# The last sequence of an attention and gated-network kernel: the order of its counts, and its third gate piece in two halves

## The chip, the cores and the metric

The kernel runs on one core of one Trainium2 chip. The metric is the device time of a run in microseconds (us); three runs of the kernel before are given, and their median is what the kernel after is compared with. All profiles here are of one execution of the program on that core.

The five engines work beside each other, each on its own queue of instructions in order: TensorE (PE in the profile, its weight loads PEld), VectorE (DVE), ScalarE (ACT), GpSimd (POOL) and SyncE (SP), which here issues most DMAs.

## What is computed

The reference, cut to what matters (B = 8 sequences of T = 512 places, E = 256, 16 heads of 16):

```python
xn = layernorm(x)
# attention: rotary positions on q and k, causal, at most 250 places back
q, k, v = split(xn @ in_proj_w.T)
attn = softmax(where(mask, rope(q) @ rope(k).T * 16 ** -0.5, min))
s = (attn @ v) @ out_proj_w.T
# gated network: weights of +1 and -1 from boolean arrays
h = s0 * (concat([xn, -xn]) @ pm1(k0));  h = relu(h) * 2
h = s1 * (h @ pm1(k1));                  h = relu(h) * 2
h = s2 * (h @ pm1(k2))
out = x + s * silu(h)
```

So the output needs, for each sequence, the attention's projection s, the gate g = h * sigmoid(h), and x itself.

## The kernel before, in words

Everything is laid out with features on the 128 partitions and the 512 places in the free dimension. Per sequence the kernel normalizes x, projects q, k and v, applies the rotation, and works through nine attention steps; each takes scores on TensorE, exponentials on ScalarE, masks on GpSimd, and the products with v on TensorE. A column of ones beside v gives the softmax sums. Meanwhile the gated network runs on TensorE: `layer` (lines 502 to 530) makes one 128-row block of h1 or h2 from a high part (16 bit) and a low part. Its `high` is a ScalarE instruction (L529) and its `low` a VectorE instruction (L527). `last` (lines 554 to 601) makes the final product z of the network, two blocks of 128 features.

**The order of the work.** The instructions of all engines are written in one order, worked out by a planner, `run` (lines 226 to 242). Pieces of TensorE work lie on a time axis with a cost each; sorted by place, they advance a clock. A piece returns follow-up steps with a delay; a step is put out as soon as the clock has passed its due time, before the next piece. A step that itself returns steps counts their delays from its own due time. Delays thus set the order in every engine's queue, and nothing is moved between queues. Each engine works its queue in that order.

**The last sequence.** In sequence 7 the network's second layer is done in two halves of 256 columns, and its output in four pieces u = 0 to 3 (`outputs`, lines 532 to 535): u = 0 and 1 are the two feature blocks of the first half of the columns, u = 2 and 3 those of the second. The pieces differ in how the gate is made:

- u = 0 and 1: `scale` (L597) copies z out of PSUM, and `gate_ready` (lines 620 to 637) follows at 7.5 and 11.0 planner units: an exponential on ScalarE (L624), an addition of 1 on GpSimd (`add`, L628), two half-width reciprocals on VectorE (`invert_`, L633), and a product on GpSimd (L635).
- u = 2 and 3 ("final"): `ends` is an exponential (L584) and an addition of 1 (L585), both on ScalarE; `ready` is one reciprocal over 256 columns (L589) and a product with z (L590), both on VectorE. The buffer `den` of u = 2 takes the place of that of u = 0 and 1 (`beside`, lines 537 to 547: one buffer per tag, pieces with odd u take the right half). The first exponential of u = 2 therefore waits until L635 of u = 1 has read it.

**The divisions.** `divisions` (lines 959 to 969) plans, for each of the two head pairs of a sequence, four reciprocals of softmax sums (`invert`, L884), and then `divide` (lines 886 to 906): a shuffle on VectorE (L890), and 2.0 units later `product` on GpSimd (L893), which divides V. `below` on GpSimd (L897) compares the sums S with a least value, and `count` on VectorE (L902) counts the sums in range into a column of `counts`. In the last sequence `below` comes 0.0 after `product`, and `count` 1.5 after `below`.

**The check and the fallback.** `add_up` (lines 973 to 978) sums all counts: a product with ones on TensorE (L975, into a PSUM buffer of the same three that the projections use), a VectorE reduction (L977) and a cast (L978). At the end all engines read that number (L1025) and branch (L1072): if a sum was out of range, a plain version of the whole computation runs; with these inputs it doesn't.

**The end.** `project_o` (lines 908 to 948) makes the attention's projection for each u on TensorE (L916). For u = 0 and 3 VectorE multiplies it with the gate straight from PSUM (L938) and the residual is added on GpSimd or VectorE (L945); for u = 1 and 2 ScalarE copies it out of PSUM (L928), GpSimd multiplies (L929), and VectorE (u = 1) or GpSimd (u = 2) adds the residual (L931). Then the piece is stored, by SyncE's queue or, for u = 3, ScalarE's.

In the last sequence the places on the planner's axis, in order, are: h2 blocks f = 0 to 7 of the second half, the product of u = 2, `add_up`, the product of u = 3, and `project_o` of u = 0, 1, 2, 3. `add_up` and the steps cost the planner's clock nothing; an h2 block costs 1.725, a product of `last` 1.87, a `project_o` 0.87. The first gate product of this sequence (u = 0) is followed by the last attention step (1.7), the gate product of u = 1 (1.87), block f = 0, the last attention products (0.7), and blocks f = 1 to 7. The `divide` of the second pair stands between blocks f = 3 and f = 4.

Of the kernel before, what the change touches and what calls it, by code (L numbers as in the profile page):

```python
# [15 lines left out]
AF = mybir.ActivationFunctionType  # L16
ALU = mybir.AluOpType
# [17 lines left out]
def tile_attention_times_gated_ffn(  # L35
# [42 lines left out]
    nc = tc.nc  # L78
    P = 128
    B, T, E = x.shape  # L80
# [90 lines left out]
    scales = const.tile([P, 2], F32, name="scales")  # L171
# [360 lines left out]
    def outputs(b):  # L532

        n = 1 if b + 1 < B else 2
        return [(f, ts(half, T // n)) for half in range(n) for f in range(EC)]

    def beside(b, u, tag):

        st = states[b]
        if b + 1 == B and u % 2:  # L540
            return st[tag][:, T // 2 :]
        if b + 1 == B and u == 2 and tag == "xr":

            st[tag] = turned.tile([P, 2, T], F32, tag="mb", name=f"xr_{b}_{u}", bufs=1)[:, 0]
        else:
            st[tag] = work.tile([P, T], F32, tag=tag, name=f"{tag}_{b}_{u}", bufs=1)
        return st[tag][:, : T // 2] if b + 1 == B else st[tag]

    def residual(b, u):
        f, cols = outputs(b)[u]  # L550
        xr = states[b]["xr", u] = beside(b, u, "xr")
        nc.sync.dma_start(xr, x_t[b, ts(f, P), cols])

    def last(b, u, how):
        st = states[b]
        f, cols = outputs(b)[u]
        if how == "final":
            pz = ps_s.tile([P, 2, T], F32, tag="sc", name=f"z_ps_{b}_{u}")[:, 0, : T // 2]
        else:
            pz = ps_m.tile([P, T], F32, tag="mm", name=f"z_ps_{b}_{u}")  # L560
            if b + 1 == B:
                pz = pz[:, : T // 2]
        if how == "at once":
            for c in range(NF1):
                nc.tensor.matmul(
                    pz, w2["l"][:, c, ts(f, P)].bitcast(F32), st["h2p"][:, c, cols],
                    start=(c == 0), stop=(c == NF1 - 1),
                )
        else:
            for p in "hl":  # L570
                for c in range(NF1):
                    nc.tensor.matmul(  # L572
                        pz, w2[p][:, c, ts(f, P)], st["h2" + p][:, c, cols],
                        start=(c == 0 and p == "h"), stop=(c == NF1 - 1 and p == "l"),
                    )
        if cols.start == 0:
            st["gate of", f] = outs.tile([P, T], F32, tag=f"gate{f}", name=f"gate_{b}_{f}")
        gate = st["gate", u] = st["gate of", f][:, cols]
        if how == "final":
            residual(b, u)  # L580
            den = beside(b, u, "den")

            def ends():
                nc.scalar.activation(den, pz, AF.Exp, scale=scales[:, 1:2])  # L584
                nc.scalar.activation(den, den, AF.Identity, bias=1.0)  # L585
                return [(0.0 if u == 2 else 0.88, ready)]

            def ready():
                nc.vector.reciprocal(den, den)  # L589
                nc.vector.scalar_tensor_tensor(  # L590
                    gate, pz, scales[:, 0:1], den, ALU.mult, ALU.mult
                )

            return [(0.0, ends)]

        def scale():
            nc.vector.tensor_scalar(gate, pz, scales[:, 0:1], None, ALU.mult)  # L597
            if how != "later":
                return [(7.5 if u == 0 else 11.0, lambda: gate_ready(b, u))]

        return [(0.0, scale)]
# [18 lines left out]
    def gate_ready(b, u):  # L620
        st = states[b]
        residual(b, u)
        gate, den = st["gate", u], beside(b, u, "den")
        nc.scalar.activation(den, gate, AF.Exp, scale=-1.0)  # L624
        width = T // 2 if b + 1 == B else T

        def add():
            nc.gpsimd.tensor_scalar(den, den, 1.0, None, ALU.add)  # L628
            return [(0.9 + 1.1 * k, lambda k=k: invert_(k)) for k in range(2)]

        def invert_(k):
            part = den[:, ts(k, width // 2)]
            nc.vector.reciprocal(part, part)  # L633
            if k == 1:
                return [(1.8, lambda: nc.gpsimd.tensor_tensor(gate, gate, den, ALU.mult))]  # L635

        return [(0.5, add)]
# [17 lines left out]
    def finish_ffn(b, u, how):  # L655
        quick.add(last_at(b, u))
        out = [(last_at(b, u), L3 * (2 if b + 1 < B else 1), lambda: last(b, u, how))]
        if how == "later":
            out.append((late(b, u) - 4.5, 0, lambda: gate_ready(b, u)))
        return out  # L660
# [225 lines left out]
    def divide(b, pair):  # L886
        st = states[b]
        V, S = st["V", pair], st["S", pair]
        R = turned.tile([P, 2, T], F32, tag="hi", name=f"R_{b}_{pair}")[:, 0]
        nc.vector.stream_shuffle(R, S, [(n + D) % 32 for n in range(32)])  # L890

        def product():
            nc.gpsimd.tensor_tensor(V, V, R, ALU.mult)  # L893
            return [(3.0 if b + 1 < B else 0.0, below)]

        def below():
            nc.gpsimd.tensor_scalar(R, S, 1 / MOST, None, ALU.is_ge)  # L897
            return [(4.0 if b + 1 < B else 1.5, count)]

        def count():  # L900
            n = 2 * b + pair
            nc.vector.scalar_tensor_tensor(  # L902
                R, S, 1 / LEAST, R, ALU.is_le, ALU.mult, accum_out=counts[:, n : n + 1]
            )

        return [(2.0, product)]
# [241 lines left out]
```

## Time and profile before

| what | value |
|---|---|
| three runs, median (lowest to highest) | 607.96 us (607.72 to 608.24) |
| profiled execution, span from first to last instruction | 607.0 us |
| profiled execution's own time beyond the span | not stated by the profile |
| granted TensorE clock, mean | 0.995 |
| instructions | 11176 |
| VectorE's last instruction of the work (L945) | 600.25 to 600.74 us |
| idle of ScalarE before L584 of u = 2, released by GpSimd L635 | 2.06 us |
| L584 with 256 columns (exponential) | 473 ns |
| L585 with 256 columns (addition of 1 on ScalarE) | 416 ns |
| L589 with 256 columns (reciprocal) | 1729 and 1753 ns |
| L884 with 128 columns (reciprocal) | 893 to 954 ns |
| L897 with 512 columns (comparison on GpSimd) | 1491 to 1822 ns |
| L902 with 512 columns (count) | 681 to 940 ns |

How to read it: the span runs from the first to the last instruction of one execution, so it is a little shorter than a run's time. The timeline and the chain give starts in microseconds from the span's start. An idle time in front of an instruction names what released it; it is inferred from semaphore events. Where two timeline rows of one engine overlap by a few hundredths, the engine has them in its pipeline together.

### The profile page before, as it was taken

How to read it: one execution, taken by the hardware profiler on the slowest of the kernel's cores; microseconds unless marked ns; L12 is line 12 of the kernel's file. 1: busy time of each engine (PE TensorE's matmuls, PEld its weight loads, DVE VectorE, ACT ScalarE, POOL GpSimd, SP SyncE). 2: the span in 40 equal slices, each digit the busy share in tenths (PEclk: the TensorE clock that was granted, in tenths of full speed). 3: DMA queues.
4: the chain of work that ended last, by engine and by line, in shares of the span. 5: the costliest groups of instructions: out<-in, count | busy, mean ns of one | idle time of the engine just before them, and what ended most of it. 6: DMA issues, size and time to landing. Idle time of an engine off the chain costs nothing. (4 is left out here: it accounts for less than half of the span.)

```text
span 607.0 us, 11176 instructions
## 1 busy us (share of the span) xinstructions
PE 594.8 (98%) x4492; PEld 367.2 (60%) x4492; DVE 383.5 (63%) x606; ACT 294.7 (49%) x414; POOL 309.0 (51%) x368
## 2 busy tenths in 40 slices
PE   7999999999999999999999999999999999999994
PEld 6654666555655556556565566555666555657783
DVE  6864637558467485665856657666666557554774
ACT  4676664354554535445453454542554445555321
POOL 2975542466533663445724557235662456627632
PEclk9999999999999999999999999999999999999998
DMA  8552722226331443315243252421642216222201
GB/s 273 216 187 94 272 87 88 86 106 207 105 122 53 176 138 105 122 65 216 85 134 108 106 210 78 142 94 70 210 131 94 88 69 243 71 65 77 71 1 41
DMA packets 38061, 74.51 MB, mean 123 GB/s; under 512 B 5360, under 2 KB 13040, under 8 KB 38000
## 3 DMA queue, kind: packets, MB, share of 16 engines
q1 hardware_dynamic: 35568, 71.48, 34.0%
q10 hardware_dynamic: 2432, 2.23, 1.2%
q8 instruction: 37, 0.61, 0.4%
q14 instruction: 24, 0.20, 0.1%
HBM read 44.30 MB, written 29.39 MB: 121 GB/s over the span
## 5 line engine op out<-in xcount | busy, mean ns | idle before, releaser
L752 ACT ACTIVATE p<-sc 128x1024 f32<-128x1024 f32 (+2 forms) x144 | 138.3, 1012 | 74.9 <-PE sc L733 45.1
L768 POOL TENSOR_SCALAR_AFFINE_SELECT p<-p 128x512 f32<-128x512 f32 x128 | 91.3, 719 | 127.4 <-ACT p L752 127.4
L518 PE MATMUL h_ps<-h1l,w1l_sb 128*128 128x512 f32 (+1 forms) x576 | 146.2, 396 | 0.0
L518 PE MATMUL h_ps<-h1h,w1h_sb 128*128 128x512 f16 (+1 forms) x576 | 123.1, 356 | 0.0
L518 PEld LDWEIGHTS h_ps<-h1l,w1l_sb 128*128 128x128 f32 x576 | 100.2, 188 | 29.5 <-issue 9.2
L529 ACT ACTIVATE h2h<-h_ps 128x512 f16<-128x512 f32 (+1 forms) x72 | 39.4, 548 | 112.6 <-PE h_ps L518 112.6
L518 PEld LDWEIGHTS <-w1h_sb 128*128 128x128 f16 x576 | 51.2, 98 | 58.8 <-issue 17.5
L775 POOL TENSOR_SCALAR_AFFINE_SELECT p<-p 128x512 f32<-128x512 f32 (+1 forms) x96 | 49.3, 513 | 71.4 <-ACT p L752 71.4
L807 PE MATMUL po<-p,v_pad 128*32 128x378 f32 (+4 forms) x1216 | 76.5, 372 | 0.0
L633 DVE RECIPROCAL den<-den 128x256 f32<-128x256 f32 (+1 forms) x32 | 52.5, 1644 | 24.9 <-POOL den L628 24.9
L733 PEld LDWEIGHTS sc<-q,k 32*128 32x128 f32 x1216 | 44.2, 184 | 30.4 <-issue 21.1
L527 DVE SCALAR_TENSOR_TENSOR h2l<-h_ps,h2h 128x512 fp32r<-128x512 f32 (+1 forms) x72 | 43.8, 609 | 29.6 <-ACT h2h L529 29.6
L527 DVE SCALAR_TENSOR_TENSOR h1l<-h_ps,h1h 128x512 fp32r<-128x512 f32 x64 | 42.7, 680 | 25.7 <-ACT h1h L529 25.6
L733 PE MATMUL sc<-q,k 32*128 32x378 f32 (+4 forms) x1216 | 58.1, 306 | 0.6 <-DMA q<-dq 0.3
L884 DVE RECIPROCAL S<-S 128x128 f32<-128x128 f32 x64 | 57.5, 920 | 0.1
L518 PE MATMUL h_ps<-xl,w0l_sb 128*128 128x512 f32 x128 | 52.3, 489 | 0.0
L807 PEld LDWEIGHTS po<-p,v_pad 128*32 128x32 f32 x1216 | 31.7, 109 | 28.4 <-issue 17.0
L529 ACT ACTIVATE h1h<-h_ps 128x512 f16<-128x512 f32 x64 | 38.0, 598 | 18.7 <-PE h_ps L518 18.6
L301 DVE TENSOR_TENSOR xT<-xT,of_all 128x512 f32<-128x512 f32 x28 | 22.3, 801 | 28.4 <-DMA of_all<-d 27.9
L518 PE MATMUL h_ps<-xh,w0h_sb 128*128 128x512 f16 x128 | 38.4, 382 | 0.1
L572 PE MATMUL z_ps<-h2l,w2l_sb 128*128 128x512 f32 (+1 forms) x144 | 36.1, 391 | 0.2 <-DVE h2l L527 0.2
L425 POOL TENSOR_TENSOR m_ka<-m_ka,m_kb 128x512 f32<-128x512 f32 x16 | 20.1, 1276 | 28.5 <-DVE m_kb L404 28.5
(101 smaller groups left out, 735.1 us busy)
## 6 DMA issues: line engine op xcount, KB each, us to landing
q<-dq SPq DMA_DIRECT2D x64, 256.0 KB, 3.5
dq<-qh SPq DMA_DIRECT2D x16, 512.0 KB, 3.1
dq<-m_qa SPq DMA_DIRECT2D x16, 512.0 KB, 5.5
k<-dk SPq DMA_DIRECT2D x32, 256.0 KB, 2.7
dk<-kh SPq DMA_DIRECT2D x8, 512.0 KB, 2.9
dk<-m_ka SPq DMA_DIRECT2D x8, 512.0 KB, 2.9
x<-in_x_dram SPq DMA_DIRECT2D x30, 128.0 KB, 2.7
xT<-in_x_t_dram SPq DMA_DIRECT2D x7, 512.0 KB, 5.6
```

The costliest lines, as they stand in the source:

```text
L301: nc.vector.tensor_tensor(xT, xT, st["of_all"][:, i], op)
L518: nc.tensor.matmul(ph, w[p][:, c, ts(f, P)], st[src + p][:, c, cols], start=(k == 0), stop=(k == n - 1),)
L527: nc.vector.scalar_tensor_tensor(lo, ph, 0.0, hi, ALU.max, ALU.subtract)
L529: high = lambda: nc.scalar.activation(hi, ph, AF.Relu)
L572: nc.tensor.matmul(pz, w2[p][:, c, ts(f, P)], st["h2" + p][:, c, cols], start=(c == 0 and p == "h"), stop=(c == NF1 - 1 and p == "l"),)
L633: nc.vector.reciprocal(part, part)
L733: nc.tensor.matmul(sc[r // 2][:, r % 2, ds(off, n)], st["k0", g][row, ts(j, P)], st[f"q{turn}", g][row, ds(j * P + first, n)], start=(turn ...
L752: nc.scalar.activation(p[:, 2 * half : 2 * half + 2, :n], sc[half][:, :, :n], AF.Exp, scale=D ** -0.5,)
L768: nc.gpsimd.affine_select(out=block, in_=block, compare_op=ALU.is_ge, fill=0.0, base=0, pattern=[[0, 4], [1, P]], channel_multiplier=-1,)
L775: nc.gpsimd.affine_select(out=block, in_=block, compare_op=ALU.is_ge, fill=0.0, base=-1, pattern=[[0, 4], [-1, beyond]], channel_multiplier=1,
L807: nc.tensor.matmul(po[32 * r : 32 * r + 32, ds(j * P + first, n)], v_columns(j, g, r), p_[:, r, ds(off, n)], start=(j == 0), stop=(done an ...
L884: nc.vector.reciprocal(part, part)
```

## The change

Three delays and one step of the last sequence change; other sequences keep their instructions and their order.

- In `product` and `below`, for the second pair (pair = 1) of the last sequence, the delay before `below` goes from 0.0 to 2.5 and that before `count` from 1.5 to 2.5. The first pair keeps 0.0 and 1.5.
- `ends` of u = 2 makes two exponentials of 128 columns on ScalarE and no addition. `ready` of u = 2 makes, for each half, the addition of 1 on VectorE and then the reciprocal. u = 3 stays as it was.
- `ready` of u = 2 comes 0.1 after `ends` instead of 0.0. `add_up`, which has the next place on the axis, is then put out ahead of `ready`.

```diff
+            halves = [ts(k, T // 4) for k in range(2)]
+
             def ends():
+                if u == 2:
+                    for k in halves:
+                        nc.scalar.activation(
+                            den[:, k], pz[:, k], AF.Exp, scale=scales[:, 1:2]
+                        )
+                    return [(0.1, ready)]
                 nc.scalar.activation(den, pz, AF.Exp, scale=scales[:, 1:2])
                 nc.scalar.activation(den, den, AF.Identity, bias=1.0)
-                return [(0.0 if u == 2 else 0.88, ready)]
+                return [(0.88, ready)]
 
             def ready():
-                nc.vector.reciprocal(den, den)
+                if u == 2:
+                    for k in halves:
+                        nc.vector.tensor_scalar(den[:, k], den[:, k], 1.0, None, ALU.add)
+                        nc.vector.reciprocal(den[:, k], den[:, k])
+                else:
+                    nc.vector.reciprocal(den, den)
                 nc.vector.scalar_tensor_tensor(
                     gate, pz, scales[:, 0:1], den, ALU.mult, ALU.mult
                 )
...
         def product():
             nc.gpsimd.tensor_tensor(V, V, R, ALU.mult)
-            return [(3.0 if b + 1 < B else 0.0, below)]
+            return [(3.0 if b + 1 < B else 2.5 * pair, below)]
 
         def below():
             nc.gpsimd.tensor_scalar(R, S, 1 / MOST, None, ALU.is_ge)
-            return [(4.0 if b + 1 < B else 1.5, count)]
+            return [(4.0 if b + 1 < B else 1.5 + 1.0 * pair, count)]
```

## The prediction

> **What bounds the kernel now.** I read the page's busy shares first, then the chain that ended last in order of time, then the timeline of the last 18 us, then the end-of-program entries of the trace.
>
> The busy shares (busy us, share of the span, instructions):
>
> ```profile
> PE 594.8 (98%) x4492; PEld 367.2 (60%) x4492; DVE 383.5 (63%) x606; ACT 294.7 (49%) x414; POOL 309.0 (51%) x368
> ```
>
> TensorE carries the kernel until the matmuls run out. All that the diff touches lies in the last sequence, after about 586 us, where the order is different. The chain (start us, us, what):
>
> ```profile
> 589.11 1.36 POOL den L628
> 590.47 2.24 issue
> ...
> 593.49 0.48 ACT den L584
> ...
> 594.51 1.76 DVE den L589
> ...
> 600.25 0.49 DVE gate L945
> ```
>
> See that the chain begins on GpSimd, not on TensorE: the second gate's addition (L628) is late, its two reciprocals (L633) and multiplication (L635) follow, and only then does ScalarE start the third piece's exponential (L584), since it overwrites the den buffer that L635 reads. From 594.51 to 600.74 VectorE works with no gap. Why L628 is late, and what else stands in a row, is in the timeline (start us, us, engine, line, operation):
>
> ```profile
> 587.54 1.49 POOL L897 TENSOR_SCALAR R<-S 128x512 f32<-128x512 f32 x1
> ...
> 589.06 0.69 DVE L902 SCALAR_TENSOR_TENSOR R<-S,R 128x512 f32<-128x512 f32 x1 [2.36 <-POOL R L897]
> ...
> 592.92 0.38 PE L572 MATMUL z_ps<-h2l,w2l_sb 128*128 128x256 f32 x1 [0.20 <-DVE h2l L527]
> ...
> 596.92 1.59 PEld L916 LDWEIGHTS att_ps<-V,wo_sb 128*128 128x128 f32 x8 [0.23 <-DVE found_f L977]
> ```
>
> The comparison L897 holds GpSimd until 589.03 although L628's input is there at 586.26 (ScalarE L624, 585.85 + 0.41). The count L902 waits for L897 and holds up the lows (L527) behind it; at 592.92 TensorE itself waits 0.20 for the last low, and at 596.9 another 0.23 for L977, whose PSUM buffer it needs. After the last addition the program branches around its fallback:
>
> ```profile
> L1072 DVEq COMPARE_BRANCH  x1: 76/76/76, 601.0 to 601.0; - x1
> L1072 SPq COMPARE_BRANCH  x1: 45/45/45, 601.2 to 601.2; - x1
> L1072 ACTq COMPARE_BRANCH  x1: 54/54/54, 601.7 to 601.7; - x1
> ...
> L1072 DVEq EVENT_SEMAPHORE  x1: 21/21/21, 605.6 to 605.6; - x1
> L1072 ACTq EVENT_SEMAPHORE  x1: 17/17/17, 605.7 to 605.7; - x1
> ```
>
> So 6.26 us (600.74 to 607.0) follow VectorE's last instruction: a store (issue 0.37 from 600.78), the branch, about 4 us until the engines go on, and the closing.
>
> **What the Trainium skill says.** (1) "SBUF — State Buffer", section "SBUF: two separate sides": a VectorE instruction with two SBUF inputs and a GpSimd one exclude each other. The trace agrees: L628 with 256 columns took 0.85 in its first run and 1.36 beside L902. (2) "VectorE: DVE Perf Modes", "The perf-mode tier table": a 32-bit tensor_scalar in SBUF can go at two elements a cycle. The trace's nearest, L311 (256 columns, operands from SBUF), took 0.41, and L256 with 2 to 4 columns 0.17, which is one a cycle; none with an immediate and many columns on VectorE, in SBUF, is in the trace. (3) "Runtime: NRT & Kernel Launch", "Instruction fetch mechanics": a taken branch out of the fetched window waits for a DMA of instructions. The trace agrees: 2.8 to 4.6 us from branch to next entry (GpSimd 600.1 to 602.9, VectorE 601.0 to 605.6).
>
> **Part 1: comparison and count later (L897, L902).** I followed the planner's clock by hand. With c the clock after the h2 pieces f5, f6, f7 (16.49, 18.215, 19.94 in units counted from the last sequence's first gate piece), product is due at 15.04, the second gate's addition at 16.94, its reciprocals at 17.84 and 18.94, its multiplication at 20.74. Before: comparison 15.04, count 16.54. After: 17.54 and 20.04. So GpSimd's order becomes L893, L628, L897, L635, and the count passes low f5, L633, low f6, L633, low f7 on VectorE; 20.04 against 19.94 is a thin but certain order. Nothing is added or dropped, and no DMA moves.
> GpSimd: L893 ends 587.45, L628 587.54 to 588.39 (0.85, as no L902 is beside it; 1.36 if a low disturbs it), L897 588.4 to 589.9 (1.49; the trace has up to 1.82). VectorE: low f5 at 587.81 (its high ends 587.78) instead of 589.7; L633 588.42 to 589.37; low f6 after the high of f6 (589.22 + 0.38): 589.63 to 589.99; L633 to 590.96; low f7 after high f7 (591.05 + 0.38): 591.46 to 591.82; count 591.8 to 592.5 with its accumulator read. L635 runs 591.1 to 591.8. Thus TensorE no longer waits at 592.7: z of u=2 ends at 591.66 + 1.18 = 592.84, and ScalarE starts at 592.87 instead of 593.49. The work that hides L897 now is the lows and reciprocals up to 591.8; 1.9 us of slack, so even 1.36 for L628 and 1.82 for L897 (+0.84) cost nothing. Behind the count wait the sum matmul L975 and behind it z of u=3: TensorE reaches L975 at about 592.7, the counts are there at about 592.55. Cover 0.1 to 0.2 only; a slow L902 (longest in the trace 0.94, +0.25) would push L975 and L977 by about 0.1.
>
> **Part 2: sum ahead of the reciprocals (L975, L977, L978).** The third piece's ready step gets a delay of 0.1 and so falls past add_up: L977 and L978 now come before it. L975 at 592.7 to 592.95, L977 593.0 (0.16), L978 593.2 to 593.31, next VectorE instruction at 593.33. The first exponential half is ready at 593.24, so this costs 0.06 to 0.1 in front and takes L977 and L978 out of the row between L590 and L938: L590 to L938 was 0.67 (596.30 to 596.97), and becomes about the 0.40 of L590's pitch, gain 0.27. TensorE's 0.23 wait for L977 goes too. L975 and z of u=3 move up by about 0.55, so its exponential (now 595.40) starts at 594.83 and its den is ready at 595.8.
>
> **Part 3: the third piece in halves.** ScalarE loses L585 (0.42) and has two exponentials of 128 columns: L529 gives 0.384 at 256 and 0.596 at 512 columns, so 0.106 less than L584's 0.473, 0.367 each; first one 592.87 to 593.24, second done by 593.6. VectorE gains two additions and has two reciprocals for one. Additions: not in the trace at this size. Lower bound 0.17 (L256, nearly no columns), upper 0.41 (L311, double columns); I take 0.27, near 0.29 for one element a cycle. Reciprocals: 0.90 each (L884 pairs, 1.76 for two) against 1.75. So L590 starts at 593.33 + 2 x (0.27 + 0.04 + 0.90 + 0.02) = 595.79, against 596.30: gain 0.51.
> The second half's exponential is hidden under the first half's reciprocal (0.9 against 0.37). The halves count as apart: at 595.40 ScalarE wrote the other half of this same buffer while L589 was at work.
>
> **Sum.** 0.51 up to L590 and 0.27 behind it: 0.78 at L938. Then L589 of u=3 needs its den at 596.5 (there at 595.8), L931 needs GpSimd's L929, whose row starts with L938 as before and whose copies come from a TensorE that is 0.5 to 0.8 earlier: no new wait. L945 ends 599.96 instead of 600.74. The stores and the branches of SP, VectorE and ScalarE move by the same 0.78, if the tail keeps its 6.26. The trace doesn't state its execution's own time; span 607.0 lies 0.96 under the median of the three runs, 607.96 (607.72 to 608.24), and I keep that 0.96 for what is around it. Span 606.22, time **607.2**, that is 0.13% less.
>
> **Rivals.**
> A, the forecast: 0.4 to 1.1 us off, 606.85 to 607.55. The ends are the additions' bounds (0.17 gives 0.98, 0.41 gives 0.50) and 0.1 for the count.
> B, the VectorE row eats most of it: additions of 0.41, reciprocals of 0.95 as two of L633 were, the count 0.2 late, or halves that wait for both exponentials (0.3). Gain 0.1 to 0.3, time 607.75. For it: the thin cover of the count. Against: the 0.17 fixed part leaves little room.
> C, slower: the branch. Counts summed early let TensorE and SP read the total sooner, and TensorE, GpSimd, VectorE and ScalarE branch in other places between the stores. One restart took 4.6, another 2.8; an engine that now takes 4.0 and meets the stores' packets (16 DMA engines up to 90% busy at 601 to 602.7) can take longer. From 0.78 more on it eats the gain; with 1.5 more, 608.7. Against: all these fetches already lie among stores, and all shift together.
> D, the same spread the other way: ScalarE and VectorE restart in about 3 us, as GpSimd did. One more us off: 606.2.
>
> **Numbers.** A 0.62, B 0.20, C 0.08, D 0.10. The range, 606.7 to 608.1, holds A and B and leaves out most of C and D. Chances of faster by over 0.2% (1.2 us, about what a measurement of this kernel can tell from no change; under 606.74): 0.11, D and a rest of A. Slower by over 0.2% (over 609.2): 0.03, the far part of C. Within: 0.86.
>
> **What would show it.** L628 starts before L897 at about 587.5; TensorE's wait at 592.9 is gone; the first L584-like exponential starts at 592.9, released by TensorE and not by L635; L977 starts at about 593.0, and no L916 wait for it; L590 of u=2 starts at about 595.8, L938 at 596.2, L945 ends at about 600.0. If additions measure over 0.45, or L977 starts after 593.4, B holds. If L945 ends at 600.0 but the span is not near 606.2, it is C or D. The prediction is wrong at its root if ScalarE's third exponential still waits for L635.

## The result, and the profile after

The kernel after takes 607.11 us (median of 21 runs, 606.51 to 608.32), the kernel before 607.85 (21 runs beside them). The ratio is 0.9985 with a 95% interval of 0.9979 to 0.9990: 0.1% to 0.2% faster. Forecast were 607.2 and a range of 606.7 to 608.1. Two later measurements of the same pair gave 0.9978 (0.9969 to 0.9987) and 0.9984 (0.9978 to 0.9991). The gain is small, but all three intervals leave out no change.

The profiled execution of the kernel after has a span of 604.9 us and a time of 606.62. Its busy shares hardly differ from before:

```profile
PE 593.5 (98%) x4492; PEld 366.9 (61%) x4492; DVE 384.1 (64%) x609; ACT 294.2 (49%) x414; POOL 312.9 (52%) x368
```

The diff adds 13 lines in front of all that follows it, so L897, L902, L628, L977, L938, L945 and L1072 of before are L910, L915, L641, L990, L951, L958 and L1085 here. In the step of u = 2 the exponentials are L588, the additions L599, the reciprocals L600 and the product L603. The timeline of the kernel after (start us, us, engine, line, operation, idle before it and releaser):

```profile
587.19 0.86 POOL L641 TENSOR_SCALAR den<-den 128x256 f32<-128x256 f32 x1
588.13 1.49 POOL L910 TENSOR_SCALAR R<-S 128x512 f32<-128x512 f32 x1
...
590.64 1.05 PE L572 MATMUL z_ps<-h2h,w2h_sb 128*128 128x256 f16 x8
...
591.44 1.18 PE L572 MATMUL z_ps<-h2l,w2l_sb 128*128 128x256 f32 x8
...
592.20 0.08 DVE L915 DVE_READ_ACCUMULATOR R<-S,R 128x1 f32 x1
...
592.56 0.21 PE L988 MATMUL total<-counts,ones 128*1 128x24 f32 x2
...
592.72 0.62 ACT L588 ACTIVATE den<-z_ps,scales 128x128 f32<-128x128 f32 x2 [1.50 <-PE z_ps L572]
...
592.80 0.17 DVE L990 TENSOR_REDUCE found_f<-total 1x1 f32<-1x24 f32 x1 [0.52 <-PE total L988]
593.01 0.14 DVE L991 CAST whole<-found_f 1x1 int32<-1x1 f32 x1
593.12 0.23 DVE L599 TENSOR_SCALAR den<-den 128x128 f32<-128x128 f32 x1
593.38 0.95 DVE L600 RECIPROCAL den<-den 128x128 f32<-128x128 f32 x1
594.25 0.16 DVE L599 TENSOR_SCALAR den<-den 128x128 f32<-128x128 f32 x1
594.45 0.95 DVE L600 RECIPROCAL den<-den 128x128 f32<-128x128 f32 x1
595.44 0.48 DVE L603 SCALAR_TENSOR_TENSOR gate<-z_ps,scales,den 128x256 f32<-128x256 f32 x1
595.84 0.41 DVE L951 TENSOR_TENSOR gate<-att_ps,gate 128x256 f32<-128x256 f32 x1
...
599.14 0.50 DVE L958 TENSOR_TENSOR gate<-gate,xr 128x256 f32<-128x256 f32 x1
```

The same places before:

```profile
590.86 1.05 PE L572 MATMUL z_ps<-h2h,w2h_sb 128*128 128x256 f16 x8
...
593.49 0.47 ACT L584 ACTIVATE den<-z_ps,scales 128x256 f32<-128x256 f32 x1 [2.06 <-POOL gate L635]
...
596.30 0.48 DVE L590 SCALAR_TENSOR_TENSOR gate<-z_ps,scales,den 128x256 f32<-128x256 f32 x1
596.70 0.16 DVE L977 TENSOR_REDUCE found_f<-total 1x1 f32<-1x24 f32 x1
...
596.97 0.40 DVE L938 TENSOR_TENSOR gate<-att_ps,gate 128x256 f32<-128x256 f32 x1
```

See four things. The addition L641 runs ahead of the comparison and takes 0.86, not 1.36. The eight matmuls of z stand in one piece of 1.18, where before the eighth waited for a low. ScalarE's exponential is released by TensorE and no longer by GpSimd's product. And L990 and L991 lie in front of the gate's additions, so that L951 can follow L603 at once.

The executions start their last part at different times, so I measure from the first matmul of z of u = 2. From there to the end of the last addition it is 599.64 - 590.64 = **9.00** us, against 600.74 - 590.86 = **9.88** before. This "distance" has lost 0.88, and what lies behind the last addition went from 6.26 to 604.9 - 599.64 = 5.26. The second of these needs its own explanation, since the change has nothing in it that should shorten the end. The end of the kernel after, in the entries of its branch:

```profile
L1085 SPq COMPARE_BRANCH  x1: 45/45/45, 599.8 to 599.8; - x1
L1085 DVEq COMPARE_BRANCH  x1: 76/76/76, 599.8 to 599.8; - x1
L1085 ACTq COMPARE_BRANCH  x1: 54/54/54, 600.7 to 600.7; - x1
...
L1085 DVEq EVENT_SEMAPHORE  x1: 21/21/21, 603.1 to 603.1; - x1
L1085 ACTq EVENT_SEMAPHORE  x1: 17/17/17, 604.0 to 604.0; - x1
```

VectorE goes on 3.3 after its branch, not 4.6 as before; ScalarE 3.3, not 4.0.

### The profile page after: what moved, and what is told of

The parts are those of the page before. It is cut to its first block, busy times and chain, and to the rows that moved or that the text cites. A ratio compares the mean times of both kernels' runs of the same rounds, so it can differ in the third digit from the quotient of the medians.

```text
span 604.9 us, 11178 instructions
## 1 busy us (share of the span) xinstructions
PE 593.5 (98%) x4492; PEld 366.9 (61%) x4492; DVE 384.1 (64%) x609; ACT 294.2 (49%) x414; POOL 312.9 (52%) x368
## 4 chain that ended last, share of the span: by engine, by line
PE 94%; DVE 2%; POOL 1%; DMA 1%; ACT 0%; issue 0%; ACTq 0%; DVEq 0%
PE h_ps L518 48%; PE po L820 12%; PE z_ps L572 9%; PE sc L746 9%; PE v_ps L365 4%; PE att_ps L929 4%; PE ka_ps L388 2%; PE qa_ps L388 2%; PE kb_ps L388 2%; PE qb_ps L388 2%; DMA wqkv_sb<-in_w_qkv_dram 1%; POOL m_qa L425 1%; POOL m_ka L425 0%; POOL w1l_sb L194 0%; DVE m_qa L449 0%
## 5 line engine op out<-in xcount | busy, mean ns | idle before, releaser
L781 POOL TENSOR_SCALAR_AFFINE_SELECT p<-p 128x512 f32<-128x512 f32 x128 | 94.9, 748 | 125.7 <-ACT p L765 125.6
L897 DVE RECIPROCAL S<-S 128x128 f32<-128x128 f32 x64 | 57.5, 920 | 0.1
L301 DVE TENSOR_TENSOR xT<-xT,of_all 128x512 f32<-128x512 f32 x28 | 23.7, 848 | 26.1 <-DMA of_all<-d 25.6
```

The source lines that it names most:

```text
L781: nc.gpsimd.affine_select(out=block, in_=block, compare_op=ALU.is_ge, fill=0.0, base=0, pattern=[[0, 4], [1, P]], channel_multiplier=-1,)
```

## The experiments

All profiles in one table, in us; "end" is from the end of the last addition to the end of the span.

| kernel | first matmul of z, u = 2 | distance | end | span |
|---|---|---|---|---|
| before; again; a third time | 590.86; 591.28; 591.05 | 9.88; 9.89; 9.87 | 6.26; 5.73; 5.08 | 607.0; 606.9; 606.0 |
| order alone | 590.62 | 9.34 | 5.24 | 605.2 |
| sum alone | 590.78 | 9.64 | 5.58 | 606.0 |
| halves alone | 590.81 | 9.86 | 6.13 | 606.8 |
| order and sum | 590.61 | 9.08 | 5.61 | 605.3 |
| after; again; a third time | 590.64; 591.65; 590.76 | 9.00; 9.00; 9.00 | 5.26; 5.35; 5.24 | 604.9; 606.0; 605.0 |
| late count | 590.76 | 10.38 | 5.86 | 607.0 |
| tangent | 591.05 | 8.48 | 5.47 | 605.0 |
| tangent, store by SyncE | 590.57 | 8.49 | 5.94 | 605.0 |
| no branch | 591.52 | 9.00 | 2.78 | 603.3 |

My theory: VectorE's row (its instructions one behind the other) in the last ten microseconds carries the gain, term by term (theory 1). The first rival: the gain is scatter in the engines' restart after the branch. The second: of the three parts, one gives nothing.

### Order alone

```diff
-            return [(3.0 if b + 1 < B else 0.0, below)]
+            return [(3.0 if b + 1 < B else 2.5 * pair, below)]
-            return [(4.0 if b + 1 < B else 1.5, count)]
+            return [(4.0 if b + 1 < B else 1.5 + 1.0 * pair, count)]
```

> Part 1 alone: the second pair's comparison and count later (delays 2.5 and 2.5), nothing else. Measure: the distance from the first matmul of z of u = 2 to the end of the last addition L945, 9.88 us before (590.86 to 600.74) and 9.00 after (590.64 to 599.64). Theory 1, the row of VectorE carries the gain: the exponential of u = 2 is released by TensorE at about 2.05 and not by L635 at 2.63, everything behind it moves by about 0.6, distance 9.26 to 9.3, time about 0.6 below the kernel before. Rival, the gain is scatter of the restart after the branch: the distance still shrinks, but the time stays within 0.2 of before.

Distance 9.34, so 0.54 off; the exponential starts 2.08 after the first matmul of z, released by TensorE:

```profile
592.70 0.47 ACT L584 ACTIVATE den<-z_ps,scales 128x256 f32<-128x256 f32 x1 [1.50 <-PE z_ps L572]
```

The gain is 0.04 to 0.08 less than theory 1 said. The time doesn't settle it: median 607.72 against 608.07 in these runs, 0.35 less, but a ratio of 1.0006 (0.9997 to 1.0015), whose interval leaves out a gain of 0.54 us (0.9991). I take the distance as shown, and what reaches the time from this part alone as open.

### Sum alone

```diff
-                return [(0.0 if u == 2 else 0.88, ready)]
+                return [(0.1 if u == 2 else 0.88, ready)]
```

> Part 2 alone: ready of u = 2 gets the delay 0.1, so the sum of the counts (L977, L978) comes ahead of the reciprocal; order of the comparison and the one whole reciprocal as before. Theory 1: L977 and L978 run while VectorE waits for ScalarE anyway (it idles 1.65 before L589), so they leave the row at no cost: distance 9.60, time 0.25 to 0.3 below before; TensorE's 0.23 wait for L977 is gone. Rival: the sum now waits for TensorE or for the counts and takes the place in front of the reciprocal, distance 9.85 or more, no gain.

Distance 9.64, 0.24 off, 0.04 less than theory 1 said. The ratio of 1.0004 (0.9994 to 1.0014) can't tell 0.24 us from nothing (median 607.95 against 608.07). The sum of this kernel runs under ScalarE's work:

```profile
593.40 0.17 DVE L977 TENSOR_REDUCE found_f<-total 1x1 f32<-1x24 f32 x1 [0.61 <-PE total L975]
593.61 0.14 DVE L978 CAST whole<-found_f 1x1 int32<-1x1 f32 x1
594.44 1.75 DVE L589 RECIPROCAL den<-den 128x256 f32<-128x256 f32 x1 [0.69 <-ACT den L585]
```

VectorE still idles 0.69 for L585 after the cast: here the sum costs nothing.

### Halves alone

The kernel after with the delays of before; the diff is against the kernel after:

```diff
-                    return [(0.1, ready)]
+                    return [(0.0, ready)]
-            return [(3.0 if b + 1 < B else 2.5 * pair, below)]
+            return [(3.0 if b + 1 < B else 0.0, below)]
-            return [(4.0 if b + 1 < B else 1.5 + 1.0 * pair, count)]
+            return [(4.0 if b + 1 < B else 1.5, count)]
```

> Part 3 alone: halves of u = 2 with the additions on VectorE; comparison, count and sum ordered as before. Theory 1: the first half's exponential (0.37 in place of 0.47 + 0.42) lets VectorE start 0.55 sooner, but two additions (0.23 and 0.16) and 0.14 more of reciprocals with their gaps follow on VectorE: L590 comes 0.05 to 0.15 sooner, distance 9.75 to 9.85, time within 0.2 of before. Rival, the halves are the main gain as the prediction's part 3 has it when it credits them with 0.5 at L590: distance 9.4 to 9.5.

Distance 9.86: 0.02 off, about the scatter of the distance itself and a little under the 0.03 to 0.13 that theory 1 gave. The time shows no gain either (ratio 1.0005, 0.9998 to 1.0011). The rows of this kernel:

```profile
593.83 0.23 DVE L599 TENSOR_SCALAR den<-den 128x128 f32<-128x128 f32 x1 [1.02 <-ACT den L588]
...
596.23 0.48 DVE L603 SCALAR_TENSOR_TENSOR gate<-z_ps,scales,den 128x256 f32<-128x256 f32 x1
```

VectorE starts 3.02 after the first matmul of z, where the whole reciprocal of before started at 3.65, 0.63 later. But it needs 2.40 until the product and not 1.79. The halves move ScalarE's addition onto the engine that is in short supply. Alone they give nothing that can be measured, as the second rival has it.

### Order and sum, without the halves

The edits of the first two kernels together.

> Parts 1 and 2 without part 3 (one exponential, the addition on ScalarE, one whole reciprocal). Theory 2: with L977 and L978 in front of it VectorE can't begin before about 2.48 in either form, and whole it ends as soon: exponential 2.08 to 2.55, addition to 3.0, reciprocal 3.05 to 4.8, L590 at 4.82 against 4.80 in the kernel after. Distance 9.0 to 9.05, time equal to the kernel after within 0.2, so the halves give nothing. Rival, the halves count: distance 9.3 or more and time 0.3 to 0.5 above the kernel after.

Distance 9.08 against 9.00: the halves are worth 0.08 on top of the other two parts, where at most 0.05 was expected. Time: median 607.31 against 608.07, ratio 0.9992 (0.9983 to 1.0001). It wasn't timed beside the kernel after, and 0.08 us is beneath what the times show. The whole form of the same stretch:

```profile
592.97 0.14 DVE L978 CAST whole<-found_f 1x1 int32<-1x1 f32 x1
593.71 1.75 DVE L589 RECIPROCAL den<-den 128x256 f32<-128x256 f32 x1 [0.60 <-ACT den L585]
595.50 0.48 DVE L590 SCALAR_TENSOR_TENSOR gate<-z_ps,scales,den 128x256 f32<-128x256 f32 x1
```

VectorE idles 0.60 for L585, which the halves fill with work; nearly all of that work is their own extra cost.

### A late count

The kernel after with later delays; the diff is against the kernel after:

```diff
-            return [(3.0 if b + 1 < B else 2.5 * pair, below)]
+            return [(3.0 if b + 1 < B else 6.0 * pair, below)]
-            return [(4.0 if b + 1 < B else 1.5 + 1.0 * pair, count)]
+            return [(4.0 if b + 1 < B else 1.5 - 1.0 * pair, count)]
```

> The kernel after with the comparison of the second pair put behind the second gate's product L635 (delays 6.0 and 0.5 in place of 2.5 and 2.5): the count is late on purpose. It prices the cover that the prediction calls thin. Theory 1: the comparison runs from 0.97 to 2.46 on this clock, the count to 3.2, TensorE stands at the sum's product until 3.2 (2.0 before) and z of u = 3 with it, L977 and L978 end at 3.75 in place of 2.5, and the row moves by 1.2: distance 10.2 to 10.3, time 1.2 above the kernel after, so slower than the kernel before by 0.4. Rival, the counts are waited for only at the very end: distance stays within 0.2 of 9.00.

Distance 10.38, 1.38 more than the kernel after and 0.08 above the range expected. The ratio to the kernel before is 1.0002 (0.9991 to 1.0012): the whole gain is gone; median 608.78 against 607.38 of the kernel after on the same chip, 1.40 more. TensorE's row shows where it stands:

```profile
591.56 1.18 PE L572 MATMUL z_ps<-h2l,w2l_sb 128*128 128x256 f32 x8
594.06 0.21 PE L988 MATMUL total<-counts,ones 128*1 128x24 f32 x2 [1.31 <-DVE R L915]
594.20 1.05 PE L572 MATMUL z_ps<-h2h,w2h_sb 128*128 128x256 f16 x8
```

So the sum in front of the last product of the network is a real wait in TensorE's queue. In the kernel after it isn't met: the counts are there at 592.28 (L915's accumulator, 592.20 + 0.08), TensorE comes at 592.56. That is 0.28 apart. In the late kernel 0.06 passes between the end of the count (594.00) and the sum (594.06), so about 0.22 of it is slack.

### Before and after once more

> The kernel before once more, unchanged, for a second profile of its end. Theory 1, what follows L945 is scatter of stores and restarts that has nothing to do with the row: distance 9.88 again, and an end behind L945 that can lie anywhere from 5.2 to 6.3. Rival, the change shortened the end too: 6.1 to 6.3 again, as in the first profile of before and in the kernel with the halves alone (6.13).

> The same a third time. Theory 1: distance 9.88, end behind L945 from 5.2 to 6.3, not the same as in the second profile. Rival: 6.1 to 6.3 in all three.

> The kernel after once more, unchanged, on the chip of the other kernels of this call: a second profile of its end, and its time beside theirs. Theory 1: distance from the first matmul of z of u = 2 to the end of L945 is 9.00 again, since nothing in that row is left to chance; time 0.6 to 0.9 below the kernel before. On the end behind L945 (6.26 us in the profile of before, 5.26 in the first profile of after): if it belongs to the kernel it is 5.2 to 5.4 again; if it is scatter of stores and restarts it can be anything from 5.2 to 6.3.

The distance repeats to 0.02 in the kernel before and doesn't move at all in the kernel after. The end doesn't repeat: 6.26, 5.73 and 5.08 before, 5.26, 5.35 and 5.24 after. The third profile of before has a shorter end than any of after. So the 1.00 that the first two profiles differ by behind the last addition is no fixed effect of the change. The means, 5.69 and 5.28, are of three profiles each and can't exclude that a few tenths of it are; the start of the last part scatters by 1.0 us too (590.64 to 591.65).

### Without the branch

The kernel after, cut behind the last store: the counts are summed, but no engine reads the total, and the fallback is left out of the program.

```diff
-    found = nc.values_load(whole[0:1, 0:1], min_val=0, max_val=n_rows)
...
-    with tc.If(found < n_rows):
...
```

> The kernel after without the branch and the fallback: the counts are still summed, but no engine reads the total, and the plain version of the computation is left out of the program. It shows what the 5.3 to 6.3 us behind L945 are. Theory 1, the restart of the engines after the branch ends last (ScalarE's entry at 4.4 to 5.0 behind L945 in all profiles so far): without it the end behind L945 shrinks by 1 to 2 us to the landing of the stores and the closing, time 1 to 2 below the kernel after. Rival, the landing of the last stores ends last: the end stays 5.2 or more, time within 0.3 of the kernel after. Distance 9.00 in both.

The end shrinks from 5.35 to 2.78, and the time from 607.38 to 604.97 on the same chip, by 2.41 (ratio to before 0.9938, 0.9923 to 0.9953). That is more than the 1 to 2 that theory 1 gave it. The mean granted clock of this profile is 1.000 against 0.997, but that is no cause: up to 602 us both have 1.00, and they differ only behind the last matmul. What SyncE waits for at the end of this kernel (engine, line, what it waited for: us in total, times, longest):

```profile
SPq L1092 <- DMA out_dram<-gate: 1.5, 3, 0.7
```

Here the landing of the stores ends last. With the branch it is the engines' restart. In the thirteen profiles with a branch the last entry of SyncE or ScalarE behind it comes 4.3 to 5.0 us after the last addition, and the span ends 0.8 to 1.4 after that entry. Which of the two is last changes: in the first profile of before SyncE took 3.8 us to go on, in the other two 2.9, and there it then waited 0.8 and 0.2 for ScalarE.

### Gates from a tangent

The rows point at the reciprocals. z * sigmoid(z) is 0.5 z (1 + tanh(z / 2)), which needs none. The order is that of the kernel after; the diff is against the kernel before, and cut:

```diff
-        nc.vector.tensor_scalar(scales[:, 1:2], scales[:, 0:1], -1.0, None, ALU.mult)
+        nc.vector.tensor_scalar(scales[:, 1:2], scales[:, 0:1], 0.5, None, ALU.mult)
...
             def ends():
+                nc.scalar.activation(den, pz, AF.Tanh, scale=scales[:, 1:2])
+                return [(0.1 if u == 2 else 0.88, ready)]
...
             def ready():
+                nc.vector.scalar_tensor_tensor(gate, den, 1.0, pz, ALU.add, ALU.mult)
```

In `project_o` all four pieces are then multiplied from PSUM by VectorE, those of u = 2 and 3 with the half scale.

> The kernel after, with the gates of u = 2 and 3 from a hyperbolic tangent, z * sigmoid(z) = 0.5 z (1 + tanh(z / 2)): one ScalarE instruction and one VectorE instruction for each, no reciprocals; all four pieces multiplied from PSUM by VectorE (L938), residual on GpSimd but for u = 3. Theory 1, VectorE's row is what ends last: it loses 2 x 0.95 + 0.39 + 1.74 of reciprocals and additions, and TensorE's last projection (ending at 7.50) comes to end last; L945 ends at 7.5 + 0.03 + 0.42 + 0.5 = 8.45 to 8.5 against 9.00; time about 0.5 below the kernel after. Rival, ScalarE must change its function table between the exponentials and the tangents (the one table load in the profile takes 1.28): 1.3 or more is added, distance above 9.5.

Distance 8.48, and one table load in the whole profile, at the start. VectorE now waits for TensorE's projection:

```profile
594.93 3.62 PE L912 MATMUL att_ps<-V,wo_sb 128*128 128x256 f32 x16
...
598.58 0.48 DVE L919 SCALAR_TENSOR_TENSOR gate<-att_ps,scales,gate 128x256 f32<-128x256 f32 x1 [0.38 <-PE att_ps L912]
599.10 0.43 DVE L930 TENSOR_TENSOR gate<-gate,xr 128x256 f32<-128x256 f32 x1
```

The matmuls end at 598.55, the addition at 599.53. The time is 607.24 beside 607.38 of the kernel after (ratios to before 0.9977, 0.9967 to 0.9987, and 0.9978): the 0.52 of the row, which was expected in the time, doesn't show there, and why stays open. The second step gave the last store to SyncE:

```diff
-            adder, queue = (nc.vector, nc.scalar) if very_last else (nc.gpsimd, nc.sync)
+            adder, queue = (nc.vector, nc.sync) if very_last else (nc.gpsimd, nc.sync)
```

> The kernel with the tangent (e5) and the last store, that of u = 3, issued by SyncE in place of ScalarE. Theory 1: L945 ends at 8.48 again; ScalarE, whose entry behind the branch was the last in all profiles with a branch (4.3 to 5.0 behind L945), branches some 4 us sooner, and SyncE's and VectorE's entries (2.9 to 4.4 and 3.5 to 4.9) come to end last: end behind L945 4.7 to 5.2, time 0.2 to 0.5 below the kernel with the tangent, and 0.8 to 1.2 below the kernel after. Rival: the entries of VectorE and SyncE scatter as far as ScalarE's, and nothing is gained behind L945 that the times can tell: 0.4 to 0.6 below the kernel after, from the row alone.

> The kernel after a third time, for the comparison with the kernel of the tangent and the store of SyncE on the same chip. Theory 1: distance 9.00, end behind L945 from 5.1 to 6.3, time 0.7 to 1.2 below the kernel before. Rival, the first ratio of 0.9985 was the true one and the second of 0.9978 its scatter: the two intervals overlap (0.9979 to 0.9990 and 0.9969 to 0.9987), and this one falls between.

ScalarE's entry comes 1.5 ahead of the last addition's end as meant, but SyncE now branches 0.9 behind it (0.1 to 0.5 elsewhere) and goes on at 4.0; the end was 5.94. Time 606.94 (ratio 0.9983, 0.9975 to 0.9991) against 607.34 of the kernel after beside it (0.9984, 0.9978 to 0.9991). Expected were an end of 4.7 to 5.2 and a time 0.8 to 1.2 below the kernel after; both missed, and the rival, that SyncE's entries scatter as ScalarE's do, fits better. The row is shorter by 0.51, the median by 0.40; the two intervals overlap, so a gain in time over the kernel after isn't shown.

## Why the prediction was right

**Part 1, the order.** Right in its mechanism. Predicted for the start of ScalarE's exponential: 592.87, 2.01 after the first matmul of z; measured 2.08 (592.72 - 590.64). L641 at 0.86 and the comparison at 1.49 fit the 0.85 and 1.49 of the forecast. This agrees with "SBUF — State Buffer", "SBUF: two separate sides", as far as the same addition took 1.36 beside the count and 0.86 without. The cover called thin held: about 0.22, where 0.1 to 0.2 was said; its price, had it failed, is about one for one (1.31 of wait, 1.38 of distance).

**Part 2, the sum.** The predicted 0.27 is 0.24 to 0.26 (before to sum alone, 9.88 to 9.64; order alone to order and sum, 9.34 to 9.08). L977 predicted at 593.0 (2.14), measured 2.16.

**Part 3, the halves.** Here the working credits wrongly. It wrote "gain 0.51" for L590 under the halves, but that start of 593.33 needs TensorE and ScalarE as the first part leaves them; the halves alone give 0.02, and 0.08 on top of the others. The sum came out since the comparison was made against the row of before, and not part by part. Read part by part, a kernel without the halves would have been forecast to gain 0.27; its distance shrank by 0.80. The terms: additions 0.23 and 0.16 (0.27 each said), with their gaps and two reciprocals 2.32 from start to product (2.46 said), first addition at 2.48 (2.47 said).

The second addition took 0.16 for 128 columns, no more than L256's 0.17 for two to four. The estimate of 0.29, built on one element a cycle, doesn't fit this form; "VectorE: DVE Perf Modes", "The perf-mode tier table", with two elements a cycle, fits better; no run here measured the rate by itself.

**The row.** Predicted distance 599.96 - 590.86 = 9.10, measured 9.00; predicted gain 0.78, measured 0.88. Most of the 0.10 comes from the additions. The three differences of the medians, 0.74, 1.02 and 0.76, lie about it, and the kernel with the late count lost in time (1.40) what it lost in distance (1.38). So the distance accounts for the gain of the whole change. It doesn't do so part by part: of the order alone and of the tangent, with 0.54 and 0.52 less, the times don't show it. With medians that scatter so, it is partly luck that 607.2 came within 0.1 of 607.11.

**The end and the base of the sum.** Two steps were off and didn't hurt. "I keep that 0.96 for what is around it" set a profile's span beside the median of other runs; execution by execution a time is about 1.7 above its span (606.62 and 604.9 in one, 608.64 and 606.9 in another). The first profile of before thus belongs to a time of about 608.7, nearly a microsecond above its median. And "if the tail keeps its 6.26": that end was the longest of all profiles taken (5.08 to 6.26 with a branch). The sum was made as a difference against one base, so both errors cancelled.

**The rivals.** B, a row that eats the gain, is out: the additions were shorter than the value taken. C and D were right that the restart scatters: the end spreads over more than 1 us in the profiles of before alone. A change of the restart by the new order isn't seen, but three profiles of each can't exclude a few tenths. "Runtime: NRT & Kernel Launch", "Instruction fetch mechanics", names the fetch at a taken branch as a stall, and the kernel without the branch ends 2.4 sooner. The trace agrees that instructions are fetched there: the instruction queues move 9 packets between the last addition and the end in the kernel after, and none without the branch. That the fetch itself is what takes the time was not isolated from reading the total.

## What to carry to other kernels

In the last microseconds, write down each engine's row from a fixed event (here the first matmul of the last stage but one), and compare distances from there: they repeated to 0.02 us where times scattered by 1 to 3. A shorter distance is not yet a shorter time; time the whole as well. Cost each part of a change alone as well as in the sum, since a part can seem to earn what another earned. A check that is summed early costs nothing as long as its inputs come ahead of the queue that it is put into; know that slack, as the one kernel that overran it paid the excess in full.

## What the runs showed that was not expected

- A branch at the end that isn't even needed costs 2.4 us of 607, more than all of this change: 604.97 against 607.38, where the reading of the total and the fallback's instructions are left out with it.
- An addition of 128 columns of 32 bits in SBUF with an immediate took VectorE 0.16 to 0.23 us, hardly more than one of four columns (0.17).
- Exponentials and tangents beside each other made ScalarE load no second function table: the profile of the tangent has the one load at the start, as before.
- Between the second half's reciprocal and the product that follows, the pitch was 1.06 with the halves alone and 0.99 in the kernel after; the trace names no wait for the 0.07, and it stays open.
